# First layer of a two-layer model on one core: the first batch's convolutions moved among all batches' norms, routing and sends in one piece behind them, zeros later, a series fused

## The chip, the core and the metric

The kernel runs on one NeuronCore of one Trainium2 chip, in fp32 throughout. The metric is the device time of one execution in microseconds. The engines are TensorE (PE, with its weight loads PEld), VectorE (DVE), ScalarE (ACT), GpSimd (POOL) and SyncE (SP). Each takes its instructions in order; DMAs are issued from the queues of SP, ACT and POOL.

## What is computed

The input `u` is 8 batches of 512 rows of 256. Two layers follow, each `x + attention(norm(x)) + ffn(norm(x))`:

```
xn = layernorm(x)
# first layer, attention: a two-way state-space block
z, xBC, dt = split(xn @ in_proj_w.T)
dt  = softplus(dt + dt_bias)                # 16 step sizes per row
xBC = silu(causal_conv4(xBC) + conv_b)      # 1024 channels
x, B, C of both directions = split(xBC)
Y   = ssd(x * dt, -exp(A_log) * dt, B, C, chunk=128)     # both directions
y   = (shifted Y of both + x * (x @ fc_D_w.T + D)) * silu(z)
out = rmsnorm(y) * norm_w @ out_proj_w.T
# first layer, ffn: top-1 of 8 experts, each row goes to one
g, e = max, argmax of softmax(xn @ Wr + br)
out += g * (relu(xn @ W1[e] + b1[e]) @ W2[e] + b2[e])
# second layer: attention of 16 heads over a latent k and v with a decay band,
# and a top-2 mixture of 7 experts and a no-op with 512 places each
```

## The kernel before

**First stage.** `steps()` runs `norm_and_project` over the 8 batches. For one batch it takes the statistics of 4 tiles of 128 rows on DVE (L134, L135), the root on ACT (L164) with a Newton step on DVE (L169 to L174), normalises (`xn`, L140), transposes on PE into `xT` (L147, copied out by ACT at L148), multiplies with `w_small` (`pp`, L152) and copies the result into `proj` (L156): 16 step-size columns and 8 router logits. SP loads the batches (`ask`, L304) and stores each `xT` to DRAM (`keep`, L366). ACT's queue writes zeros over the expert rows' array `xd0`, a part per batch (`clear`, L121). Behind the loop come the step sizes: softplus as a series in `z2` (L391 to L406), then `da` (L412). This part and all up to L1050 is put in order by the framework's scheduler, which may interleave what is independent.

**First batch.** `first = batch[0]` loads its `xT` back from DRAM (L741). A convolution (`conv`, L751) is a projection of 128 channels on PE (`pj`, L746), a scaled copy `cv` on ACT (L755), three taps on DVE that read `pj` in PSUM (L759), `th` on ACT (Tanh, L763) and a last product on DVE (L764). There are two `pj` banks. Eight convolutions make `x` (`x_part`) and `bc` (`bc_part`) of a batch. The list `pending` with `slot()` runs the later parts of a convolution at the next call. `decays`, `tokens`, `edges` and the first parts of `chunk[0]` prepare the loop.

**Chunk loop.** 64 chunks follow (8 per batch: 4 in each direction) in an order written out by hand (`tc.manual_schedule`). Per chunk POOL makes `au` (L922), `xdd` (L965), a part of `yT` (L996) and the state (L1008); PE makes `seg` (L938), `yd` (L976), `yoff` (L994), `sp` (L1002); ACT the exponentials (L946, L947, L951); DVE `mt` (L970) and others. `others(n)` adds the next batch's convolutions and the last batch's output. Between these, `fill` takes pieces from one generator:

```
rows, rest = itertools.chain(route0(), blocks()), late()
```

A chunk pulls 4 pieces, the first two of a batch 5, the last eight 6. `route0` has 6 pieces of routing (softmax, first maximum, ranks with two matmuls L208 and L209, places, `slot0` at L442, `w_idx` at L454) and 16 pieces of two sends each: an indirect DMA from POOL's queue writes 128 rows of `xn` to their places in `xd0` (L459). `blocks` has 196 pieces for 39 blocks of 128 rows. Each block gathers its expert's weights with indirect DMAs from POOL's queue (L524), turns its rows (L540) and multiplies (`h_ps` L559, `y_ps` L577). `late` then brings the experts' rows back, makes the second layer's norm and router logits (L603 to L666), batch by batch as batches are finished; what is left of it runs inside the second layer.

**Second layer.** A loop over 128 steps of attention with its expert work between (L1464 on).

The functions that the change touches:

Of the kernel before, what the change touches and what calls it, by code (L numbers as in the profile page):

```python
# [2 lines left out]

# [50 lines left out]
def bc(ap, axis, shape):  # L54

    return ap.unsqueeze(axis).to_broadcast(shape)
# [3 lines left out]
def tile_kernel(ctx: ExitStack, tc: tile.TileContext, t, out: bass.AP):  # L60
# [57 lines left out]
    def clear(dst, rows, lo, hi):  # L118

        n = rows // P  # L120
        A.dma_start(  # L121
            out=dst[: n * P, :].rearrange("(p r) d -> p r d", p=P)[:, lo:hi, :],
            in_=bc(zero[:, : dst.shape[1]], 1, [P, hi - lo, dst.shape[1]]),
        )


    def norm_and_project(x_of, xn, xT_of, w_proj, n_proj, proj, pool, bank):

        for b in range(B):
            x = x_of(b)  # L130
            mv = pool.tile([P, TPB, 2], FP, name="mv", tag="mv")
            for c in range(TPB):
                st = pool.tile([P, 6], FP, name="st", tag="st", bufs=4)
                V.bn_stats(st, x[:, c, :])  # L134
                V.bn_aggr(mv[:, c, :], st)  # L135
            ve = pool.tile([P, TPB], FP, name="ve", tag="ve")
            V.tensor_scalar(ve, mv[:, :, 1], EPS, None, ALU.add)
            rs = rsqrt(pool, ve, [P, TPB])
            for c in range(TPB):
                V.tensor_scalar(  # L140
                    xn[:, b * TPB + c, :], x[:, c, :], mv[:, c, 0:1], rs[:, c : c + 1], ALU.subtract, ALU.mult
                )
            xT = xT_of(b)
            for k in range(KC):
                tp = bank("tp", [P, S], 0)
                for c in range(TPB):
                    T.transpose(tp[:, c * P : (c + 1) * P], xn[:, b * TPB + c, k * P : (k + 1) * P], ident)  # L147
                A.copy(xT[:, k, :], tp)  # L148
            pp = bank("pp", [P, TPB, n_proj], 1)
            for c in range(TPB):  # L150
                for k in range(KC):
                    T.matmul(  # L152
                        pp[:, c, :], xT[:, k, c * P : (c + 1) * P], w_proj[:, k, :],
                        start=(k == 0), stop=(k == KC - 1),
                    )
            V.tensor_copy(proj[:, b * TPB : (b + 1) * TPB, :], pp)  # L156

    def rsqrt(pool, v, shape):

# [201 lines left out]
    def steps():  # L361
# [3 lines left out]
        def keep(b):  # L365
            Y.dma_start(out=xtd[b], in_=xTs[b])  # L366

        def x_of(b):
            if b:
                keep(b - 1)  # L370
            if b >= 2:
                ask(b)

            n = NBLK // B + 1
            clear(xd0, NBLK * P, b * n, min(NBLK, (b + 1) * n))
            if b == 3:
                Y.dma_start(out=w_in, in_=t["w_in"])
            if b == 5:
                Y.dma_start(out=w_out, in_=t["w_out"])
            return us[b]  # L380

        def xT_of(b):
            xTs[b] = m2.tile([P, KC, S], FP, name="xT", tag="xT")
            return xTs[b]

        norm_and_project(x_of, xn, xT_of, w_small, 2 * NH + NE, proj, pool, bank)
        keep(B - 1)

# [6 lines left out]
        V.tensor_tensor(z, z, u, ALU.mult)  # L397
        V.tensor_tensor(z2, z, z, ALU.mult)
        acc = u
        V.tensor_scalar(acc, z2, 1.0 / 17.0, 1.0 / 15.0, ALU.mult, ALU.add)  # L400
        for k in range(13, 0, -2):
            V.tensor_tensor(acc, acc, z2, ALU.mult)
            V.tensor_scalar(acc, acc, 1.0 / k, None, ALU.add)
        V.tensor_tensor(acc, acc, z, ALU.mult)
        V.tensor_scalar(acc, acc, 2.0, None, ALU.mult)
        V.scalar_tensor_tensor(dt.rearrange(f2), v.rearrange(f2), 0.0, acc.rearrange(f2), ALU.max, ALU.add)  # L406
        ea = big.tile([P, 2 * NH], FP, name="ea", tag="ea")
        A.activation(ea, a_log, AF.Exp)
        V.tensor_scalar(ea, ea, -1.0, None, ALU.mult)
# [86 lines left out]
        A.activation(e8, ct, AF.Exp)  # L496
        Y.dma_start(out=exd.rearrange("g p l -> p g l"), in_=e8)

    steps()
    l1c = tl = w_r = rb = w_q = w_o = w_uk = w_uv = w_kv = band = slot1 = iota_n = proj1 = vt0 = qk0 = r1b = noop = None  # L500
    tls = ExitStack()
    for k in range(HC):
        V.tensor_scalar(w_out[:, k, :], w_out[:, k, :], norm_w[:, k : k + 1], None, ALU.mult)

    with ExitStack() as es:
        p1, p2, psum = m1, m2, mp
        H3 = [P, NH, P]
# [512 lines left out]
        def slot(work=None):  # L1020

            new = work() if work else None
            pending[:] = [more for more in [p() for p in pending] if callable(more)]
            if callable(new):
                pending.append(new)


        first = batch[0]
        first.load()
        for q in range(4):  # L1030
            slot(lambda: first.x_part(q))
        slot(), slot()
        first.skip()()
        first.ask(0), first.ask(1)
        for q in range(4):
            slot(lambda: first.bc_part(q))
            if q == 0:
                pending.append(first.start())
        while pending:
            slot()  # L1040
        first.tokens(0)(), first.tokens(3)()
        decays()
        chunk[0].prepare()
        chunk[0].segments()
# [8 lines left out]
        with tc.manual_schedule(engines=ENGINES):  # L1053
# [29 lines left out]
                    put(next_, "tokens", 0), put(next_, "tokens", 3), put(now, "z_part", 3)  # L1083
                return work

            rows, rest = itertools.chain(route0(), blocks()), late()

            def fill(n):
                for _ in range(n):
# [687 lines left out]
```

## Time and profile before

Three executions took 2058.74, 2060.02 and 2069.62 us (median 2060.02). The profiled execution took 2070.49 us, its span is 2068.8 us, and its mean granted TensorE clock 0.942.

| engine | busy us | share of the span | instructions |
|---|---|---|---|
| PE | 1840.4 | 89% | 11760 |
| PE weight loads | 1229.3 | 59% | 11760 |
| DVE | 1436.3 | 69% | 3311 |
| ACT | 1174.8 | 57% | 2536 |
| POOL | 628.1 | 30% | 572 |

The page gives busy time over the whole span, and the kernel is a sequence of stages with different limits, so the windows by stage say more: there the same columns stand for a stretch of time. In a timeline a row has the start and the duration in us, the engine, the line, what is written from what, and in brackets how long the engine stood idle before and what ended that.

Places in time, from the timeline: norm stage 0 to 72.9; step sizes done at 101.3; chunk 0's `yd` at 132.1; sends 150.2 to 206.7; first weight gather at 209.0; last `y_ps` begins at 884; chunk 63's `yd` at 1063; second layer from about 1100.

### The profile page before, as it was taken

How to read it: one execution, taken by the hardware profiler on the slowest of the kernel's cores; microseconds unless marked ns; L12 is line 12 of the kernel's file. 1: busy time of each engine (PE TensorE's matmuls, PEld its weight loads, DVE VectorE, ACT ScalarE, POOL GpSimd, SP SyncE). 2: the span in 40 equal slices, each digit the busy share in tenths (PEclk: the TensorE clock that was granted, in tenths of full speed). 3: DMA queues.
4: the chain of work that ended last, by engine and by line, in shares of the span. 5: the costliest groups of instructions: out<-in, count | busy, mean ns of one | idle time of the engine just before them, and what ended most of it. 6: DMA issues, size and time to landing. Idle time of an engine off the chain costs nothing.

```text
span 2068.8 us, 33318 instructions
## 1 busy us (share of the span) xinstructions
PE 1840.4 (89%) x11760; PEld 1229.3 (59%) x11760; DVE 1436.3 (69%) x3311; ACT 1174.8 (57%) x2536; POOL 628.1 (30%) x572
## 2 busy tenths in 40 slices
PE   5676999999999999987776998899999999999987
PEld 5333676766677677744544554466666666666654
DVE  4684766667485665678655776677777777787785
ACT  2243454545344454545433666677877777777775
POOL 0048644546454454555430034300000000000030
PEclk9877999999999999999776999899999999999999
DMA  7113654655455465543533253332231221213170
GB/s 264 61 46 113 209 200 159 209 182 197 145 187 193 159 218 186 158 130 113 165 127 105 96 174 130 110 98 72 68 102 36 81 79 53 81 54 103 34 163 11
DMA packets 150440, 262.34 MB, mean 127 GB/s; under 512 B 22362, under 2 KB 107213, under 8 KB 138369
## 3 DMA queue, kind: packets, MB, share of 16 engines
q1 hardware_dynamic: 112288, 139.62, 21.2%
q0 software_dynamic: 28512, 110.92, 17.3%
q10 hardware_dynamic: 9472, 9.67, 1.4%
q8 instruction: 93, 1.52, 0.3%
q14 instruction: 75, 0.61, 0.1%
HBM read 188.46 MB, written 76.68 MB: 128 GB/s over the span
## 4 chain that ended last, share of the span: by engine, by line
PE 36%; ACT 7%; DVE 4%; issue 1%; another core or an unknown queue 1%; DMA 1%; ACTq 0%; SPq 0%; DVEq 0%
PE p_ps L1493 8%; PE s_ps L1471 6%; PE o_ps L1502 6%; PE e_yp L1275 5%; PE e_hp L1262 5%; ACT s L1486 3%; ACT pT L1494 2%; PE qp L254 1%; DVE s L1478 1%; DVE s L1476 1%; PE fin L1434 1%; PE vp L269 1%; PE kp L262 1%; PE op L896 0%
## 5 line engine op out<-in xcount | busy, mean ns | idle before, releaser
L1476 DVE TENSOR_SCALAR s<-s_ps 128x512 f32<-128x512 f32 x512 | 318.1, 683 | 208.0 <-PE s_ps L1471 181.1
L1486 ACT ACTIVATE s<-s,ng 128x512 f32<-128x512 f32 x512 | 355.8, 727 | 5.7 <-DVE ng L1482 5.6
L1493 PE MATMUL p_ps<-ident,s 128*128 128x128 f32 x2048 | 288.6, 284 | 53.9 <-ACT pT L1494 48.9
L1478 DVE CUSTOM_DVE_ANT_0 s<-s,band 128x512 f32<-128x512 f32 x512 | 322.6, 685 | 0.0
L1493 PEld LDWEIGHTS p_ps<-ident,s 128*128 128x128 f32 x2048 | 239.0, 144 | 119.8 <-ACT pT L1494 77.5
L1494 ACT COPY pT<-p_ps 128x512 f32<-128x512 f32 x512 | 277.5, 592 | 48.3 <-PE p_ps L1493 39.2
L1281 POOL DMA_INDIRECT x<-e_yo,e_to x28 | 43.4, 1552 | 599.0 <-ACT e_yo L1280 545.8
L746 PE MATMUL pj<-xT,w_in 128*128 128x512 f32 x384 | 203.9, 658 | 17.6 <-DVE cv L759 14.7
L1471 PE MATMUL s_ps<-kT,qT 16*128 16x512 f32 x1024 | 163.6, 674 | 14.2 <-DVE s L1476 9.5
L559 PEld LDWEIGHTS h_ps<-xdT,w 128*128 128x128 f32 x1248 | 149.1, 192 | 22.4 <-issue 21.6
L559 PE MATMUL h_ps<-xdT,w 128*128 128x128 f32 x1248 | 152.7, 276 | 2.9 <-DMA w<-in_w_dram,w_idx 2.9
L759 DVE SCALAR_TENSOR_TENSOR cv<-pj,w_conv_w,cv 128x511 f32<-128x511 f32 (+2 forms) x192 | 143.0, 745 | 11.1 <-ACT cv L755 7.1
L577 PE MATMUL y_ps<-w,hT 128*128 128x256 f32 x624 | 147.3, 380 | 0.0
L922 POOL TENSOR_TENSOR au<-da,half 128x512 f32<-128x512 f32 x64 | 77.9, 1217 | 223.2 <-PE seg L938 121.1
L1502 PE MATMUL o_ps<-pT,vt 128*32 128x256 f32 x2048 | 134.0, 396 | 2.0 <-issue 1.8
L577 PEld LDWEIGHTS y_ps<-w,hT 128*128 128x128 f32 x624 | 115.9, 190 | 31.8 <-issue 17.8
L746 PEld LDWEIGHTS pj<-xT,w_in 128*128 128x128 f32 x384 | 72.1, 206 | 100.5 <-issue 91.4
L996 POOL TENSOR_TENSOR yT<-yT,ex 128x512 f32<-128x512 f32 (+1 forms) x48 | 58.6, 1220 | 222.3 <-DVE ex L995 155.1
L1262 PE MATMUL e_hp<-e_xdT,e_w 128*128 128x256 f32 x448 | 123.3, 398 | 1.5 <-ACT e_xdT L1247 0.7
L1275 PE MATMUL e_yp<-e_w,e_hT 128*128 128x256 f32 x448 | 120.4, 391 | 0.0
L951 ACT ACTIVATE mt<-seg,mid 64x64 f32<-64x64 f32 x512 | 109.8, 309 | 0.8
L763 ACT ACTIVATE th<-cv 128x512 f32<-128x512 f32 x64 | 40.3, 630 | 117.0 <-DVE cv L759 113.2
(296 smaller groups left out, 3046.6 us busy)
## 6 DMA issues: line engine op xcount, KB each, us to landing
ex<-exd SPq DMA_DIRECT2D x96, 128.0 KB
u<-in_u_dram SPq DMA_DIRECT2D x16, 512.0 KB
xtd<-xT SPq DMA_DIRECT2D x16, 512.0 KB
fr<-fdd SPq DMA_DIRECT2D x64, 128.0 KB
xT<-xtd SPq DMA_DIRECT2D x15, 512.0 KB
od<-os SPq DMA_DIRECT2D x28, 256.0 KB
e_w<-in_ei_dram SPq DMA_DIRECT2D x7, 1024.0 KB
e_w<-in_eo_dram SPq DMA_DIRECT2D x7, 1024.0 KB
```

The lines of the kernel that those rows point to most:

```text
L559: T.matmul(hp[:, i, :], w1[:, k * FF + f * P : k * FF + (f + 1) * P], xdT[:, k * P : (k + 1) * P], start=(k == 0), stop=(k == KC - 1),)
L577: T.matmul(yp, hT[f // 4][:, f % 4, :], w2[:, f * DM : (f + 1) * DM], start=(f == 0), stop=(f == FC - 1))
L746: T.matmul(pj, w_in[:, k, o * P : (o + 1) * P], self.xT[:, k, :], start=(k == 0), stop=(k == KC - 1))
L1262: T.matmul(hp, w1[:, k, f * P : (f + 1) * P], xdT[:, k, :], start=(k == 0), stop=(k == KC - 1))
L1275: T.matmul(yp, hT[:, f, c * P : (c + 1) * P], w2[:, f, :], start=(f == 0), stop=(f == FC - 1))
L1471: T.matmul(sp[i], self.q[r, cols], self.k[r, :], start=True, stop=True)
L1476: V.tensor_scalar(self.p[i], sp[i], -CLAMP, CLAMP, ALU.max, ALU.min)
L1478: V.tensor_tensor_reduce(out=self.p[i], in0=self.p[i], in1=band[:, at : at + S], scale=1.0, scalar=-3.0e38, op0=ALU.mult, op1=ALU.max, acc ...
L1486: A.activation(self.p[i], self.p[i], AF.Exp, bias=self.ng[:, i : i + 1])
L1493: T.transpose(pp[:, k, :], self.p[i][:, k * P : (k + 1) * P], ident)
L1494: A.copy(pT[i][:, :, cc * P : (cc + 1) * P], pp)
L1502: T.matmul(op[32 * i : 32 * i + 32, half * 2 * P : (half + 1) * 2 * P], self.v[:, k, h * (AD + 1) : h * (AD + 1) + 32], pT[i][:, k, :], st ...
```

## The change

- `norm_and_project` takes a function `behind(b)` that it calls after each batch. It starts two of batch 0's convolutions behind each of the batches 2 to 5. Batch 0's `xT` stays in SBUF, in a buffer of the tag `yT`, and is not loaded back.
- `route0` runs as a whole inside `steps()`, ahead of the series in the program's text, and no longer in the chunk loop's pieces.
- The zeros over `xd0` come from a tile `none`, in four DMAs behind the norm stage instead of eight in it.
- In the series, each pair of a product and an addition of a constant is one `scalar_tensor_tensor`: seven instructions fewer.
- `w_in` is asked for at batch 1 (batch 3 before, by the text), and the scaling of `w_out`, `skip`, `tokens` of chunks 0 and 3, and `start` are moved in the text.

The scheduler's order of the changed program on POOL in this stretch is: `none`, two `xdt`, 32 sends, two `xdt`, `au`, `xdd`, two `au`, two `xdt`, six weight gathers. On DVE, `slot0` stands near the end of the series, one instruction behind `da`'s first half.

```diff
@@ -124,7 +123,7 @@
         )
 
 
-    def norm_and_project(x_of, xn, xT_of, w_proj, n_proj, proj, pool, bank):
+    def norm_and_project(x_of, xn, xT_of, w_proj, n_proj, proj, pool, bank, behind):
 
         for b in range(B):
             x = x_of(b)
@@ -154,6 +153,7 @@
                         start=(k == 0), stop=(k == KC - 1),
                     )
             V.tensor_copy(proj[:, b * TPB : (b + 1) * TPB, :], pp)
+            behind(b)
 
     def rsqrt(pool, v, shape):
 
@@ -370,21 +370,43 @@
                 keep(b - 1)
             if b >= 2:
                 ask(b)
-
-            n = NBLK // B + 1
-            clear(xd0, NBLK * P, b * n, min(NBLK, (b + 1) * n))
-            if b == 3:
+            if b == 1:
                 Y.dma_start(out=w_in, in_=t["w_in"])
             if b == 5:
                 Y.dma_start(out=w_out, in_=t["w_out"])
             return us[b]
 
         def xT_of(b):
-            xTs[b] = m2.tile([P, KC, S], FP, name="xT", tag="xT")
+            if b == 0:
+                first.xT = xTs[b] = m2.tile([P, HC, S], FP, name="xT0", tag="yT")[:, :KC, :]
+            else:
+                xTs[b] = m2.tile([P, KC, S], FP, name="xT", tag="xT")
             return xTs[b]
 
-        norm_and_project(x_of, xn, xT_of, w_small, 2 * NH + NE, proj, pool, bank)
+        def behind(b):
+
+            for q in range(2 * b - 4, min(2 * b - 2, 2 * HC)) if b >= 2 else ():
+                part = first.x_part if q < HC else first.bc_part
+                slot(lambda: part(q % HC))
+            if b == B - 1:
+                while pending:
+                    slot()
+
+        norm_and_project(x_of, xn, xT_of, w_small, 2 * NH + NE, proj, pool, bank, behind)
         keep(B - 1)
+
+        none = m1.tile([P, TPB, DM], FP, name="none", tag="u", bufs=2)
+        G.memset(none, 0.0)
+        slots = xd0.rearrange("(p r) d -> p r d", p=P)
+        for lo in range(0, NBLK, 3 * TPB):
+            n = min(3 * TPB, NBLK - lo)
+            k = n // 3 if n % TPB else TPB
+            A.dma_start(
+                out=slots[:, lo : lo + n, :].rearrange("p (n k) d -> p n (k d)", k=k),
+                in_=bc(none[:, :k, :].rearrange("p k d -> p (k d)"), 1, [P, n // k, k * DM]),
+            )
+        for _ in route0():
+            pass
 
 
 
@@ -397,13 +419,13 @@
         V.tensor_tensor(z, z, u, ALU.mult)
         V.tensor_tensor(z2, z, z, ALU.mult)
         acc = u
-        V.tensor_scalar(acc, z2, 1.0 / 17.0, 1.0 / 15.0, ALU.mult, ALU.add)
-        for k in range(13, 0, -2):
-            V.tensor_tensor(acc, acc, z2, ALU.mult)
-            V.tensor_scalar(acc, acc, 1.0 / k, None, ALU.add)
-        V.tensor_tensor(acc, acc, z, ALU.mult)
+        acc, z, z2, v = (a.rearrange(f2) for a in (u, z, z2, v))
+        V.tensor_scalar(acc, z2, 1.0 / 17.0, None, ALU.mult)
+        for k in range(15, 1, -2):
+            V.scalar_tensor_tensor(acc, acc, 1.0 / k, z2, ALU.add, ALU.mult)
+        V.scalar_tensor_tensor(acc, acc, 1.0, z, ALU.add, ALU.mult)
         V.tensor_scalar(acc, acc, 2.0, None, ALU.mult)
-        V.scalar_tensor_tensor(dt.rearrange(f2), v.rearrange(f2), 0.0, acc.rearrange(f2), ALU.max, ALU.add)
+        V.scalar_tensor_tensor(dt.rearrange(f2), v, 0.0, acc, ALU.max, ALU.add)
         ea = big.tile([P, 2 * NH], FP, name="ea", tag="ea")
         A.activation(ea, a_log, AF.Exp)
         V.tensor_scalar(ea, ea, -1.0, None, ALU.mult)
@@ -496,12 +518,8 @@
         A.activation(e8, ct, AF.Exp)
         Y.dma_start(out=exd.rearrange("g p l -> p g l"), in_=e8)
 
-    steps()
     l1c = tl = w_r = rb = w_q = w_o = w_uk = w_uv = w_kv = band = slot1 = iota_n = proj1 = vt0 = qk0 = r1b = noop = None
     tls = ExitStack()
-    for k in range(HC):
-        V.tensor_scalar(w_out[:, k, :], w_out[:, k, :], norm_w[:, k : k + 1], None, ALU.mult)
-
     with ExitStack() as es:
         p1, p2, psum = m1, m2, mp
         H3 = [P, NH, P]
@@ -1026,19 +1044,16 @@
 
 
         first = batch[0]
+        steps()
         first.load()
-        for q in range(4):
-            slot(lambda: first.x_part(q))
-        slot(), slot()
+        for k in range(HC):
+            V.tensor_scalar(w_out[:, k, :], w_out[:, k, :], norm_w[:, k : k + 1], None, ALU.mult)
         first.skip()()
         first.ask(0), first.ask(1)
-        for q in range(4):
-            slot(lambda: first.bc_part(q))
-            if q == 0:
-                pending.append(first.start())
+        first.tokens(0)(), first.tokens(3)()
+        pending.append(first.start())
         while pending:
             slot()
-        first.tokens(0)(), first.tokens(3)()
         decays()
         chunk[0].prepare()
         chunk[0].segments()
@@ -1083,7 +1098,7 @@
                     put(next_, "tokens", 0), put(next_, "tokens", 3), put(now, "z_part", 3)
                 return work
 
-            rows, rest = itertools.chain(route0(), blocks()), late()
+            rows, rest = blocks(), late()
 
             def fill(n):
                 for _ in range(n):
```

More of the change, by code (lines that the diff above doesn't have):

```diff
@@ L1 @@
-import itertools
 from contextlib import ExitStack
```

## The prediction

> **What bounds the kernel now.** I read the windows by stage first, to see where TensorE has room, then the timeline of each engine's queue from 0 to 230 us, then the first starts of the groups `yd` (L976, once per chunk) and `y_ps` (L577, once per expert block). Columns: stretch, its length, busy us (instructions) of PE, weight loads, DVE, ACT, POOL, then granted clock, DMA share, GB/s.
>
> ```profile
> 0.00:76.00 76.00, 48.58 (x197) 41.80 (x198) 35.87 (x167) 16.62 (x31) 3.30 (x20) 1.00 0.64 221
> 76.00:101.00 25.00, 12.66 (x21) 3.48 (x19) 24.55 (x40) 5.62 (x9) 0.00 (x0) 0.78 0.01 1
> 101.00:132.00 31.00, 20.82 (x61) 8.85 (x60) 23.80 (x33) 16.36 (x39) 10.19 (x8) 0.78 0.15 47
> 132.00:226.00 94.00, 65.66 (x270) 35.68 (x270) 53.04 (x103) 29.66 (x79) 66.20 (x64) 0.75 0.37 128
> 226.00:889.00 663.00, 649.04 (x3950) 469.36 (x3948) 437.51 (x730) 319.49 (x871) 338.37 (x292) 1.00 0.55 180
> 889.00:1063.00 174.00, 134.99 (x692) 85.06 (x690) 125.64 (x250) 80.43 (x192) 79.98 (x74) 0.86 0.46 141
> ```
>
> From 226 to 889 PE is the bound (98% busy): chunks 6 to 51 at 663/45 = 14.73 us each, with 4.25 pieces of expert work per chunk. After 889 the expert blocks are finished; twelve chunks take 14.5 us each beside the second layer's row work, DVE 72% busy. Before 226 each of the six chunks takes 15.7 us without expert work: POOL, 66.2 of 94 us busy, carries the sends (L459) between its chunk work. All the room for this change is before 226 and, through what moves out of it, after 889; the second layer from 1100 on is untouched.
>
> ```profile
> 64.74 0.26 DVE L156 COPY proj<-pp 128x96 f32<-128x96 f32 x1 [3.46 <-PE pp L152]
> 65.91 1.38 DVE L140 TENSOR_SCALAR xn<-u,mv,rq_r 128x256 f32<-128x256 f32 x4
> 72.62 0.26 DVE L156 COPY proj<-pp 128x96 f32<-128x96 f32 x1 [5.33 <-PE pp L152]
> 100.51 0.76 DVE L412 TENSOR_TENSOR da<-dt,ea 128x256 f32<-128x256 f32 x2
> 132.10 1.98 PE L976 MATMUL yd<-mt,xdt 128*64 128x128 f32 x16 [4.18 <-DVE mt L970]
> 149.71 0.18 DVE L442 CAST slot<-so_sa 128x32 int32<-128x32 f32 x1
> 163.52 0.99 POOL L459 DMA_INDIRECT xd<-xn,slot  x1 [0.17 <-issue]
> 164.82 0.98 POOL L459 DMA_INDIRECT xd<-xn,slot  x1 [0.30 <-issue]
> 208.98 1.06 POOL L524 DMA_INDIRECT w<-in_w_dram,w_idx  x1 [1.24 <-DMA xd<-xn,slot]
> ```
>
> Seen here, in time: a batch's turn in the norm stage is a latency chain of 7.88 us (64.74 to 72.62), 6.7 of it from the start of `xn` to the copy of `proj`. Step sizes are done at 101.3, chunk 0 multiplies at 132.1, slots are known at 149.9, one send occupies POOL for 1.29 us (163.52 to 164.82), and the first weight gather issues at 208.98, after the last send.
>
> **The change part by part**, against this execution. The order of the changed kernel's instructions is known: it interleaves the eight convolutions of batch 0 with the norms of batches 2 to 7, and on POOL it puts two `xdt`, then all 32 sends in one run, and only then chunk 0's `au` and `xdd`.
>
> *Convolutions moved into the norm stage.* One is three taps and a finish on DVE (rows 0.74, spaced 0.66, and 0.69), 0.78 + 0.63 on ACT, 1.9 on PE. DVE gets 8 x 2.6 = 21 us, beside 36 it has there now. The chain does not hide them, because DVE runs in order and they stand between a `proj` copy and the next `xn`. Walking it: batch 2's `u` is asked for behind batch 1's store, at 19 instead of 13.4, and is there by about 27 (8.9 us from issue now); two convolutions with a table load and three waits on ACT put `xn` of batches 2 and 3 at 37 and 39, their `proj` at 43 and 49. Batch 4: five taps 3.3, a finish 0.6, statistics and Newton 2.6, then the 6.7 chain: 62.4. Batch 5: four taps 2.6, 1.5, 6.7, and 1.0 for `fp` matmuls ahead of its `pp`: 74.3. Batch 6: three taps 2.0, statistics, Newton and a `w_out` scaling 3.4, 6.7: 86.5. Batch 7, partly ahead: 6.6, so the stage ends at 93 instead of 73. In return the stretch from 76 to 125, where these convolutions alternated with the series, keeps only the series.
>
> Sqrt and Tanh now alternate, with about ten more table loads on ACT. The row for one is
>
> ```profile
> 7.11 1.28 ACT L408 ACT_TABLE_LOAD   x1
> 8.41 0.22 ACT L408 ACTIVATE ea<-w_a_log 128x16 f32<-128x16 f32 x1
> ```
>
> so 1.30 us from load to use: 13 us on an ACT that has 60 idle there, in the chain only for batches 6 and 7, inside my walk. The Trainium skill ("ScalarE: Activation LUTs", "What ACT_TABLE_LOAD costs") adds a drain of some 1.38 us to each switch. By it up to six `rq_s` would come 1.4 later: +8 us. The trace shows no such gap; I take zero and keep 8 for the range.
>
> *Zeros later.* Eight issues on ACT's queue, 5.1 MB, leave 7 to 32 us; four larger ones go out between about 83 and 91, behind a POOL memset of 128x1024 (0.31 us for 128x272, so 1.2). At the 221 to 287 GB/s seen in the first stage they take 18 to 23 us and are down by about 114, under routing; uncovered they would hold the first send as long as they are late. The early `u` loads gain bandwidth, which only matters for batches 2 and 3, and is in the walk. SP's order changes little: `w_in` keeps its place, batch 0's `xT` is no longer reloaded (0.32 of issue). I put both at zero, bounds -3 and +3.
>
> *Routing and series.* Fusing drops seven `tensor_scalar` of 0.414 (L403): -2.9 us on DVE; STT and TT cost the same (0.683 and 0.680). From 93: softmax and first maximum 5.5, ranks on PE and eviction 2.8, then series and ranks alternate: `sp_v` 0.7 and two exponentials 1.4, the reciprocal 3.35, ten fused steps and products of 0.62 spacing each and some twenty small routing rows of 0.1 to 0.4: about 20. `dt` at 121, `slot` at 122. The kernel before had step sizes at 101 and its last batch-0 convolution at 125: chunk 0 has its inputs at the same time in both.
>
> *Sends directly behind.* After two `xdt` (2.5) the 32 sends take 32 x 1.29 = 41.3: 124 to 165. In the kernel before they cost POOL the same, but spread over chunks 0 to 5. Here `au` waits behind them, and for `au` the segment matmul, its exponentials, `mt`, and `yd`: two `xdt` to 167.6, `au` 168.8, matmul 1.1, exponentials 2.9, `mt` 1.2: chunk 0 multiplies at 174 instead of 132. Three more `au`, an `xdd` and two `xdt`, each on the other engines' leave, bring the first weight gather to 178 instead of 209; its weights land 5.9 us later as now (208.98 to 214.85), at 184. Chunk 1's `yd` stands behind block 0's first matmuls on PE, and comes at about 194.
>
> *Cold TensorE.* PE has next to nothing from 95 to 180. After the similar gap at 1100:
>
> ```profile
> 1110.00:1120.00 10.00, 1.97 (x6) 1.67 (x8) 6.81 (x18) 4.95 (x7) 0.00 (x0) 0.50 0.31 105
> 1120.00:1130.00 10.00, 8.56 (x41) 5.33 (x38) 9.71 (x32) 5.98 (x11) 0.00 (x0) 0.62 0.16 54
> 1130.00:1140.00 10.00, 9.16 (x64) 5.32 (x66) 8.41 (x21) 5.84 (x11) 0.00 (x0) 0.72 0.73 262
> 1140.00:1150.00 10.00, 9.71 (x62) 5.28 (x55) 5.91 (x15) 4.91 (x10) 0.00 (x0) 0.94 0.00 0
> ```
>
> the clock took 30 us to come back: (0.38 + 0.28 + 0.06) x 10 = 7 us of PE lost. The skill ("TensorE: Matmul & The Clock Gate", Part 1) restores it after one busy window of 3.4 us: 1.7 lost. The row is nearer, since chunk 1 has the same mix of bursts: I take 6, bounds 2 and 10. So chunk 1 at 199, and with 14.73 each chunk 6 at 272, against 226: +46.
>
> *What comes back.* Routing and sends were 22 of the pieces that chunks pull (6 and 16). Without them the blocks start with chunk 0 and end at 196/4.25 = chunk 46 instead of 218/4.25 = 51. Five chunks lose their expert work. What is such a chunk worth? From 889 the windows hold 12 bare chunks and six batches of row work. A bare chunk has 8.6 us of DVE by its rows; at the 0.72 to 0.83 filling that row work leaves DVE, 10.4 to 12; two neighbours without row work stand 9 apart (996 and 1005). I take 10.4: 5 x (14.7 - 10.4) = -22, bounds -28 (9.1) and 0 (chunks no shorter, as chunks 0 to 5 were). And batch 6's row work, which now holds PE 6.2 us after the last chunk (1071.8), finds free pieces in chunks 61 to 63: -5, bounds -8 and 0.
>
> Sum: +46 - 22 - 5 = +19, say +20: 2070.5 becomes 2090. The profiled execution is 10.5 above the median of the runs, 2060.0; to that I add the same 20: **2080**.
>
> **The rivals.**
> *Tail no shorter* (25%). Late chunks are bound by waits (DVE for `yd`, PE for `mt`), not by PE, and shedding PE work gives back only a part: -4 to -12 instead of -22. Then +29 to +42, 2090 to 2102; with the drains 2110. For it: without expert work 12 chunks took 14.5 each, not less than with it. Against: they carried six batches of row work.
>
> *A draw* (17%): norm stage done by 84, tail as taken or a bit shorter: +9 or less, 2050 to 2070.
>
> *Faster* (8%): the mixed norm stage costs nothing. PE and DVE are each idle for 27 to 40 us in the first 76, and a third of its DMA bytes leave. If the convolutions fit in those gaps and it ended at 73 as now, everything behind comes 20 earlier: chunk 6 at +26; with the tail at its best, 26 - 28 - 8 = -10, 2050. It decides at a stage end of 73; later than that the run of sends is not paid for. Against: the chain and the order on DVE above.
>
> *The change doesn't do what it says*: the scheduler might have spread the sends. The order on POOL excludes it.
>
> **Numbers.** The likeliest, 50%: +10 to +30, 2070 to 2090. What this kernel's measurement can tell from no change is about 0.5%, 10 us: 2050 and 2070 are the borders. Faster 0.08, same 0.17, slower 0.75. For 8 in 10 I leave out the fastest tenth and the last tenth beyond the uncovered drains: 2054 to 2106.
>
> **What would show it.** Right: last `proj` copy at 85 to 98; `slot` near 122; 32 sends in one run of 41 us with `au` behind it; first `yd` at 165 to 182; first weight gather at 170 to 185; chunk 6 near 272; last `y_ps` near chunk 46, and from there to the last `yd` about 226 us. Wrong: `au` ahead of the sends or a first `yd` under 150; a norm stage under 78; the chunks behind the last block at 9 us or less; or a gain in the second layer, of which I expect nothing.

## The result, and the profile after

The changed kernel takes 2093.39 us (median of four runs, 2086.59 to 2096.63) beside 2061.49 for the kernel before. The ratio is 1.0128, 95% interval 1.0103 to 1.0152: by that ratio 26 us slower. (The two medians lie 31.9 apart; the ratio is what is used below.) A second measurement, on a chip where the kernel before took 2073.91, gave 1.0122 (1.0092 to 1.0152). The profiled execution after took 2086.59 us, with a span of 2084.9, 16.1 longer than the one shown of before; of that pair only the part up to the second layer is used below, for reasons given with the runs of both kernels on one chip.

The windows by stage, of the changed kernel (columns as in the prediction):

```profile
0.00:76.00 76.00, 49.53 (x185) 31.14 (x185) 48.67 (x181) 33.49 (x47) 3.48 (x21) 0.86 0.37 126
76.00:101.00 25.00, 14.32 (x54) 10.97 (x53) 13.31 (x39) 7.86 (x13) 1.09 (x1) 0.50 0.77 289
101.00:132.00 31.00, 9.79 (x31) 5.30 (x30) 25.11 (x55) 3.98 (x8) 13.51 (x13) 0.61 0.28 90
132.00:226.00 94.00, 53.95 (x297) 38.60 (x298) 25.59 (x45) 27.78 (x81) 56.41 (x54) 0.74 0.45 158
226.00:889.00 663.00, 636.03 (x3832) 454.69 (x3831) 439.60 (x723) 308.12 (x842) 339.98 (x296) 0.99 0.54 177
889.00:1063.00 174.00, 127.83 (x619) 74.90 (x618) 119.60 (x242) 87.33 (x197) 65.03 (x57) 0.81 0.35 114
```

DVE's convolution work moved into the first 76 us (48.7 us busy instead of 35.9), and ACT's doubled there. The zeros show in the second row: DMA 77% busy at 289 GB/s. In the fourth row DVE has 25.6 us of work left instead of 53.0, and is idle all the same: up to 159.7 us chunk 0 waits for POOL. The last row is the surprise. As before, it holds only chunks without expert work, eleven of them where there were twelve, and it is hardly emptier.

The timeline of the changed kernel, from DVE, POOL and PE:

```profile
82.67 0.26 DVE L155 COPY proj<-pp 128x96 f32<-128x96 f32 x1 [2.46 <-PE pp L151]
88.62 0.26 DVE L155 COPY proj<-pp 128x96 f32<-128x96 f32 x1 [5.06 <-PE pp L151]
114.27 0.68 DVE L428 SCALAR_TENSOR_TENSOR dt<-sp_v,sp_u 128x512 f32<-128x512 f32 x1
116.35 1.02 DVE L464 CAST slot<-so_sa 128x32 int32<-128x32 f32 x1
117.67 1.72 POOL L481 DMA_INDIRECT xd<-xn,slot  x1 [0.34 <-DVE slot L464]
...
158.72 0.98 POOL L481 DMA_INDIRECT xd<-xn,slot  x1 [0.30 <-issue]
161.69 1.07 POOL L940 TENSOR_TENSOR au<-da,half 128x512 f32<-128x512 f32 x1
...
171.05 1.98 PE L994 MATMUL yd<-mt,xdt 128*64 128x128 f32 x16
174.06 1.09 POOL L542 DMA_INDIRECT w<-in_w_dram,w_idx  x1 [0.15 <-issue]
180.31 3.75 PE L577 MATMUL h_ps<-xdT,w 128*128 128x128 f32 x16 [5.36 <-DMA w<-in_w_dram,w_idx]
```

The norm stage ends at 88.9 instead of 72.9. The sends hold POOL from 117.67 to 159.70, with nothing else between them; `au` of chunk 0 follows, and chunk 0 multiplies at 171 instead of 132. The weights' gather issues at 174 instead of 209.

For chunks, the clearest clock is the one addition of `yd` into `yT` that each of them makes on DVE. Its starts (us), and that of the second layer's first score matmul, for both kernels in the first profiles and in a later pair on one chip:

| | chunk 0 | 6 | 46 | 51 | 63 | second layer | end of span |
|---|---|---|---|---|---|---|---|
| before | 134.1 | 227.2 | 820.6 | 891.4 | 1069.2 | 1102.4 | 2068.8 |
| after | 173.1 | 261.9 | 854.6 | 936.6 | 1112.2 | 1136.8 | 2084.9 |
| before, again | 134.4 | 224.1 | 822.6 | 893.4 | 1073.6 | 1106.6 | 2074.7 |
| after, again | 170.6 | 260.8 | 855.9 | 936.7 | 1108.0 | 1132.0 | 2096.6 |

In the later pair the loss is 36.2 us at chunk 0, 36.7 at chunk 6, 33.3 at chunk 46, 34.4 at chunk 63, 25.4 at the second layer and 21.9 at the end. So the start costs less than the 46 predicted, and the chunks without expert work give nothing back.

### The profile page after: what moved, and what is told of

It reads as the page before. It is cut to its first block, busy times and chain, and to the rows that moved or that the text cites. A ratio compares the mean times of both kernels' runs of the same rounds, so it can differ in the third digit from the quotient of the medians.

```text
span 2084.9 us, 33314 instructions
## 1 busy us (share of the span) xinstructions
PE 1823.4 (87%) x11760; PEld 1216.1 (58%) x11760; DVE 1427.7 (68%) x3304; ACT 1188.4 (57%) x2548; POOL 628.7 (30%) x573
## 4 chain that ended last, share of the span: by engine, by line
PE 37%; ACT 6%; DVE 4%; issue 1%; DMA 1%; POOL 1%; ACTq 0%; another core or an unknown queue 0%; SPq 0%; DVEq 0%; POOLq 0%
PE p_ps L1508 8%; PE s_ps L1486 6%; PE o_ps L1517 6%; PE e_yp L1290 5%; PE e_hp L1277 5%; ACT s L1501 3%; ACT pT L1509 2%; PE qp L254 1%; DVE s L1493 1%; DVE s L1491 1%; PE fin L1449 1%; PE vp L269 1%; PE kp L262 1%; ACT e_hT L1280 0%; PE op L914 0%
## 5 line engine op out<-in xcount | busy, mean ns | idle before, releaser
L777 DVE SCALAR_TENSOR_TENSOR cv<-pj,w_conv_w,cv 128x509 f32<-128x509 f32 (+2 forms) x192 | 142.8, 745 | 8.7 <-ACT cv L773 4.7
L595 PEld LDWEIGHTS y_ps<-w,hT 128*128 128x128 f32 x624 | 115.9, 190 | 33.3 <-issue 18.7
L988 DVE TENSOR_TENSOR mt<-mt,cbm 128x1024 f32<-128x1024 f32 x64 | 82.4, 1287 | 41.9 <-ACT mt L969 41.7
```

Of the source, the lines that this page charges most:

```text
L595: T.matmul(yp, hT[f // 4][:, f % 4, :], w2[:, f * DM : (f + 1) * DM], start=(f == 0), stop=(f == FC - 1))
```

## The experiments

They ran on several chips, on which the kernel before took from 2041 to 2075 us, so only ratios to the kernel before on the same chip are compared, and starts up to the second layer.

**The run of sends.** `e1_sends_spread` leaves routing in front, and lets the chunks pull the sends again:

```
-        for _ in route0():
-            pass
+        sends = route0()
+        for _ in range(6):
+            next(sends)
...
-            rows, rest = blocks(), late()
+            rows, rest = itertools.chain(sends, blocks()), late()
```

> The changed kernel, with the 32 sends pulled by the chunks again, two to a piece (routing stays in front). Theory (the run of sends holds POOL ahead of chunk 0's au): the first yd comes 41 us earlier, at 130 instead of 171, chunk 6 near 228 instead of 261, blocks end near chunk 50; time about 2058, ratio 0.995 to 1.003 to the kernel before. Rival (chunk 0 is late because TensorE is cold or because the zeros' transfers hold everything behind them): the first yd at 145 or later, time 2075 or more.

Measured: ratio 1.0014 (1.0005 to 1.0022). POOL's and PE's timelines of this kernel:

```profile
118.98 1.48 POOL L943 TENSOR_TENSOR au<-da,half 128x512 f32<-128x512 f32 x1
133.29 1.23 POOL L484 DMA_INDIRECT xd<-xn,slot  x1 [0.19 <-issue]
...
130.26 1.97 PE L997 MATMUL yd<-mt,xdt 128*64 128x128 f32 x16 [0.45 <-DVE mt L991]
```

`au` now stands ahead of the first send, and `yd` comes at 130.3 instead of 171. The zeros were as late (issued between 77 and 87 us, and between 78 and 88 in the changed kernel). TensorE was a little warmer: its granted clock was 0.74 from 115 to 125 us and 0.69 from 125 to 130. In the changed kernel it was 0.50 from 160 to 171, where TensorE was busy for 5.1 us, so the clock is worth 2.5 us there at most. Neither is what held chunk 0 for 41 us; the run on POOL is. It accounts for 1.1% of the changed kernel's 1.3%, some 22 us. Chunk 6 comes at 231.5 and not at 228, still 30 earlier than after.

**Routing as well.** `e2_route_spread` puts routing back into the chunks too, so that only the mixed convolutions, the late zeros and the fused series are left of the change:

```
-        for _ in route0():
-            pass
...
-            rows, rest = blocks(), late()
+            rows, rest = itertools.chain(route0(), blocks()), late()
```

> The changed kernel, with routing and sends both pulled by the chunks again, as in the kernel before; mixed convolutions, late zeros and fused series stay. Theory (behind the norm stage DVE is the path, and routing is half of it there): dt near 104 instead of 114, the first yd near 118 instead of 171 and 132 in the kernel before, chunk 6 near 213, the rest as in the kernel before: time about 2046, ratio 0.990 to 0.996. Rival (the first chunks are bound by POOL's sends and by routing, whenever chunk 0 starts; what is won there is waited out before the first block): first yd early, chunk 6 at 224 or later, ratio 0.998 to 1.003.

Measured: 0.9945 (0.9926 to 0.9963), the first `yd` at 120.71, chunk 6 at 214.6. The theory holds: behind the norm stage DVE is the path. `dt` is done at 103 instead of 114 in `e1_sends_spread`, because DVE has 19 operations from the last copy of `proj` to `dt` instead of 61: routing no longer alternates with the series. Chunk 0 wins 9.6 us by it and chunk 6 16.9, and that is still there at the second layer (17.5): routing in front costs 0.7%.

**The mixing, undone.** `e3_convs_behind` keeps routing and sends in front and calls batch 0's convolutions behind the norm stage, as in the kernel before:

```
-            for q in range(2 * b - 4, min(2 * b - 2, 2 * HC)) if b >= 2 else ():
-                part = first.x_part if q < HC else first.bc_part
-                slot(lambda: part(q % HC))
...
+        for q in range(4):
+            slot(lambda: first.x_part(q))
...
+        for q in range(4):
+            slot(lambda: first.bc_part(q))
```

> The changed kernel, with batch 0's convolutions behind the norm stage again; routing and run of sends stay in front. Theory (the mixing moves DVE work, it doesn't hide it): the last proj copy at 73 instead of 89, but 21 us of convolution stand between routing's and the series' operations, so the slots come at 120 to 128 and the first yd at 172 to 182; ratio 1.012 to 1.020. Rival (the mixing costs the norm chain more than the convolutions cost behind it): slots by 112, first yd by 166, ratio under 1.010.

Measured: 1.0124 (1.0104 to 1.0143), as slow as the changed kernel. Half of each guess was right: the ratio is the theory's, the slots are the rival's. They came at 103, and the sends ran from 103.43 to 145.65. Yet the first `yd` came at 168.45, only 2.6 earlier than after. ACT's and DVE's timelines say why:

```profile
145.72 1.04 POOL L934 TENSOR_TENSOR au<-da,half 128x512 f32<-128x512 f32 x1
148.94 0.60 ACT L958 ACTIVATE mt<-seg 128x512 f32<-128x512 f32 x1 [24.60 <-PE seg L950]
...
153.09 0.63 ACT L775 ACTIVATE th<-cv 128x512 f32<-128x512 f32 x1
153.75 0.69 DVE L776 SCALAR_TENSOR_TENSOR bc<-th,cv 128x512 f32<-128x512 f32 x1 [24.84 <-ACT th L775]
```

The scheduler had put chunk 0's exponentials ahead of the last convolutions' `th` on ACT. The exponentials wait 24.6 us for `seg`, that for `au`, that for the sends, and the convolutions stand behind them. One engine's in-order wait became another's. With the run of sends in place, then, it is worth nothing to mix or not to mix.

**The parts by themselves.** `e7_mix_only` is the kernel before with the mixed convolutions alone; `e8_no_mix` is it with the late zeros and the fused series alone. The edit of the first, with what `behind` needs of the change (`w_in` asked for with batch 1, a tile of its own for batch 0's `xT`, the calls that were moved in the text; nearly all of this is in `e8_no_mix` too):

```
-        norm_and_project(x_of, xn, xT_of, w_small, 2 * NH + NE, proj, pool, bank)
+        norm_and_project(x_of, xn, xT_of, w_small, 2 * NH + NE, proj, pool, bank, behind)
```

and of the second:

```
-            clear(xd0, NBLK * P, b * n, min(NBLK, (b + 1) * n))
...
+        none = m1.tile([P, TPB, DM], FP, name="none", tag="u", bufs=2)
+        G.memset(none, 0.0)
...
-            V.tensor_tensor(acc, acc, z2, ALU.mult)
-            V.tensor_scalar(acc, acc, 1.0 / k, None, ALU.add)
+            V.scalar_tensor_tensor(acc, acc, 1.0 / k, z2, ALU.add, ALU.mult)
```

> The kernel before, with batch 0's convolutions mixed into the norm stage and nothing else of the change (zeros early, series unfused, routing and sends in the chunks). Theory (the mixing is the part that gains where nothing holds chunk 0 up behind it: it takes 21 us of DVE from behind the norm stage and puts 14 in front): first yd near 125 instead of 132, ratio 0.996 to 0.998. Rival (early zeros and mixed convolutions collide on ACT's queue and on the early loads, so that the norm stage ends past 92): ratio 0.999 to 1.003.

> The kernel before, with late zeros and the fused series but the convolutions behind the norm stage, routing and sends in the chunks. Theory (seven tensor_scalar less on DVE and nothing else): first yd at 127 to 130 instead of 132, ratio 0.997 to 1.000. Rival (the late zeros are still under way when the first send needs them): sends later than 163, ratio over 1.001.

Measured: mixing 0.9950 (0.9931 to 0.9969), the rest 0.9997 (0.9983 to 1.0011); together they make the 0.9945 of `e2_route_spread`. The mixing gains 0.5%, more than the 0.2 to 0.4% expected, and is the only part that gains: the norm stage ends later, at 82 instead of 72 to 73, and chunk 0 starts earlier, its addition at 120.5 instead of 134.4. In `e8_no_mix` `dt` is ready at 94 instead of 100, but the last convolution finishes on DVE at 124.9 (125.6 before), so chunk 0 is only 2 us early: a shorter series is worth nothing where the convolutions end later than it.

Beside these two, the norm stage of `e2_route_spread` ended at 86.9, not at 82. With late zeros the scheduler places the convolutions among the norms in another order (on DVE the two orders part in the second batch), and that took back what fusing saved. So `e12_mix_fused` is the mixing and the fused series with early zeros; against `e2_route_spread`:

```
-        none = m1.tile([P, TPB, DM], FP, name="none", tag="u", bufs=2)
-        G.memset(none, 0.0)
...
+            n = NBLK // B + 1
+            clear(xd0, NBLK * P, b * n, min(NBLK, (b + 1) * n))
```

> The kernel before with two parts of the change, the mixed convolutions and the fused series; zeros stay early, routing and sends stay in the chunks. Theory (the last two runs: with early zeros the mixed norm stage ends at 82, with late ones at 87, which is as much as the fused series saves): both savings add here, dt at 96 to 98 instead of 102, the first yd at 113 to 117, ratio 0.990 to 0.994 to the kernel before. Rival (what chunk 0 wins is waited out in the first chunks, on POOL's sends and behind routing): first yd as said, chunk 6 no earlier than 213, ratio 0.994 to 0.997.

Measured: 0.9921 (0.9904 to 0.9937), 16 us below the kernel before and the lowest ratio of all versions. DVE and PE of it, and below them DVE of `e7_mix_only`:

```profile
80.74 0.26 DVE L156 COPY proj<-pp 128x96 f32<-128x96 f32 x1 [5.06 <-PE pp L152]
96.40 0.69 DVE L420 SCALAR_TENSOR_TENSOR dt<-sp_v,sp_u 128x512 f32<-128x512 f32 x1
113.77 1.80 PE L986 MATMUL yd<-mt,xdt 128*64 128x128 f32 x16 [3.27 <-DVE mt L980]
```

```profile
81.72 0.26 DVE L156 COPY proj<-pp 128x96 f32<-128x96 f32 x1 [5.06 <-PE pp L152]
101.63 0.69 DVE L420 SCALAR_TENSOR_TENSOR dt<-sp_v,sp_u 128x512 f32<-128x512 f32 x1
```

Behind a mixed norm stage the series is the path, and fusing it takes 4.2 us off: from the end of the last copy to the end of `dt` it is 16.1 us instead of 20.3. Chunk 46 comes at 804.7 instead of 811.5. The ratio's interval just overlaps that of `e7_mix_only`, so the whole time alone does not show the step; the starts do. It overlaps that of `e2_route_spread` as well: that early zeros are better than late ones here is likely, not shown.

**The chunks at the end.** The prediction let five more chunks lose their expert work and become 4.3 us shorter each. `e4_bare_tail` is the changed kernel with all row work (the second layer's norms and router logits, made batch by batch) held back until the last chunk is through:

```
             def fill(n):
                 for _ in range(n):
-                    if next(rows, "end") == "end":
-                        next(rest, None)
+                    next(rows, None)
...
             slot()
+            for _ in range(80):
+                next(rest)
             batch_done = B
```

> The changed kernel, with the second layer's row work of batches 0 to 6 held back until the last chunk is through, so that the chunks behind the last expert block (47 to 63) carry nothing else. Theory of the prediction (a bare chunk costs 10.4 us): from chunk 46 to chunk 63 about 180 us instead of 257. Rival (the chunks have a chain of their own that is as long with or without other work, some 14 to 15 us): 235 us or more. The whole time grows by the uncovered row work, 50 to 120 us.

Measured, in one run: 163.5 us from chunk 46 to chunk 63, where the theory had 180; chunk 47 comes at 868.0, chunk 63 at 1018.1. The additions on DVE of chunks 47 to 49 and 63:

```profile
868.01 0.68 DVE L1003 TENSOR_TENSOR yT<-yT,yd 128x508 f32<-128x508 f32 x1
876.25 0.68 DVE L1003 TENSOR_TENSOR yT<-yT,yd 128x512 f32<-128x512 f32 x1
884.73 0.69 DVE L1003 TENSOR_TENSOR yT<-yT,yd 128x512 f32<-128x512 f32 x1 [2.07 <-PE yd L994]
...
1018.15 0.68 DVE L1003 TENSOR_TENSOR yT<-yT,yd 128x508 f32<-128x508 f32 x1 [0.69 <-PE yd L994]
```

A chunk that carries nothing else, a bare chunk, takes 150.1/16 = 9.4 us, less than the prediction's 10.4. The rival that a chunk's own chain is 14 us long is out. The windows of this kernel show what becomes of the row work by itself:

```profile
868.00:1018.00 150.00, 122.71 (x677) 70.36 (x675) 109.04 (x152) 78.40 (x213) 76.71 (x62) 0.95 0.18 54
1018.00:1147.00 129.00, 68.32 (x274) 51.96 (x275) 54.88 (x180) 24.20 (x41) 36.15 (x39) 0.61 0.57 182
```

It takes 128.5 us from the last chunk to the second layer (1018.1 to 1146.6), at a clock of 0.61. No engine is busy for more than 53% of it, so none of them sets its length by itself. And bare chunks and row work one after the other take little longer than side by side. From chunk 46 to the second layer it is 292 us here, and 282 and 276 in the two profiles of the changed kernel, where the same row work lies beside the chunks. Only 10 to 16 of its 128 us were hidden there.

The whole time was 2080.9 on a chip where the kernel before took 2042.4. Against the changed kernel, at its ratio of 1.0122 to 1.0128, that is a growth of some 13 us, where I had expected 50 to 120 from row work in the open.

`e5_rows_from_52` lets the row work begin with chunk 52, close to where it began in the kernel before:

```
-                    if next(rows, "end") == "end":
+                    if next(rows, "end") == "end" and late_from <= 0:
                         next(rest, None)
...
+                late_from = 52 - n
```

> The changed kernel, with the second layer's row work allowed to start with chunk 52 only, near where it started in the kernel before; chunks 47 to 51 are bare. Theory (row work costs a chunk its slack whenever it is there, some 15 to 16 us a chunk for 4 pieces or for 6; without it a chunk takes 9.4, as the held-back run showed): chunks 46 to 51 take 47 to 55 us instead of 82, the next twelve as many as in the kernel before (178); time 18 to 30 us below the changed kernel, ratio 0.998 to 1.005 to the kernel before. Rival (each piece of row work costs about 1 us wherever it is put): what chunks 47 to 51 win is paid later, ratio 1.009 to 1.014.

Measured: 1.0189 (1.0174 to 1.0205). My theory fell. Chunks 46 to 51 took 52.4 us instead of 82, as it said, but the next twelve took 195.5 instead of 176, the end behind them 33.6 instead of 24.6, and the second layer began at 1136.7, where it began after. All that the bare chunks won was paid later, and some more: the ratio is 0.6% above the changed kernel's. Against `e8_no_mix`, traced on the same chip and as fast as the kernel before, the second layer begins 32.7 us later; the pair of before and after on one chip, below, has 25.4 there. Of these 7 us, 5 lie between chunk 46 and the second layer (281.5 us, and 276.1 in that pair); the rest of the 0.6% is not explained.

`e6_dense_tail` is `e2_route_spread` with the row work from chunk 56 on and eight pieces a chunk:

```
-                if n >= N - 8:
-                    fill(2)
+                if n >= N - 8:
+                    fill(4)
...
+                late_from = N - 8 - n
```

> The version with routing and sends in the chunks (mixed convolutions, late zeros, fused series), with the row work allowed to start with chunk 56 only and then at eight pieces a chunk instead of six. Theory (a chunk that carries row work takes some 15 us whether it carries 4, 6 or 8 pieces): chunks 52 to 55 shrink from 15 to 10 us each, the rest stays: 15 to 22 us below that version, ratio 0.984 to 0.988 to the kernel before. Rival (cost by the piece): chunks 56 to 63 grow to 17 to 18 us each and eat it: ratio 0.993 to 0.997.

Measured: 1.0061 (1.0042 to 1.0080), 1.2% worse than `e2_route_spread`. Chunks 52 to 56 shrank to 11.0 us each, and chunks 56 to 63 grew from 14.9 to 21.4, more than the rival's 17 to 18: both guesses missed. Crowded into eight chunks, row work is hidden less than in twelve.

Is it TensorE's wait for the row work's `xn`? `e9_rows_apart` is the changed kernel with two empty pieces more between `xn` and its transposes:

```
                 ahead(3)
                 yield
+                if b < 6:
+                    yield
+                    yield
```

> The changed kernel, with two empty pieces more between the normalised rows xn and the transposes that read them, in the row work of batches 0 to 5. Theory (in the tail, TensorE stands in its order before transposes whose xn is not ready, 21 us in all, and the chunks behind it stand too; that wait makes row work cost as much beside chunks as by itself): PE's wait for xn falls under 8 us, chunks 46 to 63 take 258 less 15 to 20 us, ratio 0.992 to 0.995 of the changed kernel, so 1.004 to 1.009 to the kernel before. Rival (another engine's order, or the cold clock, is what holds the chunks; the wait moves elsewhere): the wait for xn goes, the chunks take 250 us or more, ratio 1.010 to 1.016.

Measured: 1.0089 (1.0057 to 1.0121), beside 1.0122 for the changed kernel on the same chip. The waits from chunk 46 to 63, of the changed kernel and then of this one (us in total, times, longest):

```profile
PE tp L672 <- DVE xn L664: 20.9, 5, 9.4
POOL au L940 <- PE seg L956: 51.5, 9, 15.6
```

```profile
PE tp L675 <- DVE xn L664: 14.1, 4, 10.4
POOL au L943 <- PE seg L959: 48.9, 9, 21.9
```

The wait shrank by 6.8 us, not to under 8, and the stretch by 3.4 (248.7 instead of 252.1). The intervals overlap, so a gain is not shown. Two thirds of the wait are left, so it is not ruled out either, but a third of it gone gave back 3.4 us. POOL's wait for the segments, and with it the next chunk's `au`, stayed.

**Both kernels on one chip.** `e10_before_again` and `e11_after_again` are the two kernels themselves.

> The kernel before itself, for a trace beside those of the experiments. Theory (the second layer is untouched): from the second layer's first score matmul to the end 933 to 940 us, as in the experiments on this chip, not 966 as in the first profile; chunks as in the first profile. Rival (the change's gain of some 18 us in the second layer between the first two profiles is real): 950 us or more.

> The changed kernel itself, beside the experiments on their chip. Theory: ratio 1.010 to 1.015 again, and the second layer 933 to 940 us long. Rival (the first ratio was that chip's): ratio under 1.008.

Measured: from the first score matmul to the end of the span 968.1 us before and 964.6 after; `e9_rows_apart` on the same chip has 962.8. The 933 to 940 that I wrote down held for `e1_sends_spread`, `e2_route_spread` and `e3_convs_behind` on theirs (934.8, 934.9, 936.6). So that length goes with the chip (or with the hour: each chip was used once), and hardly with the kernel: within a chip it differs by 5.3 us at most. In the first two profiles it was 966.4 and 948.1, which made the changed kernel look 18 us better there. Before and after on one chip show 3.5. The ratio was confirmed.

## Why the prediction was right or wrong, point by point

- **Forecast.** 2080 was forecast and 2093.39 measured, inside the range of 2054 to 2106 and just beyond the likeliest 2070 to 2090; as a difference, 20 and 26. The direction rests on the right cause, the run of sends. That the size fits is luck. In the pair on one chip, the front was taken 9 us too dear (+46 for +36.7 at chunk 6) and the tail 23 too cheap (-22 for +1.1), and three small terms came out better than forecast: 3.4 us in the expert blocks, 4.0 in batch 6's row work, 3.5 in the second layer.
- **The walk through the norm stage** said `proj` copies at 43, 49, 62.4, 74.3, 86.5 and 93 for batches 2 to 7. They came at 43.6, 47.1, 59.6, 70.4, 82.7 and 88.6. (The steps given for batch 4 add up to 62.2; nothing hangs on it.) That DVE's order makes the stage longer was right. From a copy of `proj` to the next batch's `xn` it took 5.7, 3.9 and 4.8 us in front of batches 4, 5 and 6, with DVE busy all the time from 60 to 65 us and for 4.6 of the 5 us from 70 to 75; in the kernel before it was 0.5 to 2.0. The granted clock fell too, to 0.50 from 75 us on, where the kernel before had 1.00, but the stage's matmuls do not show it. The last batch's `pp`, before and after:

```profile
68.91 3.67 PE L152 MATMUL pp<-w_w_small,xT 128*128 128x24 f32 x16 [0.51 <-ACT xT L148]
```

```profile
84.92 3.67 PE L151 MATMUL pp<-w_w_small,xT 128*128 128x24 f32 x16 [0.51 <-ACT xT L147]
```

  The rival of a stage that ends at 73 is out. In the second profile it ended at 87.
- **Table loads.** ACT has 14 in the first 90 us instead of 4: ten more, as said. One of the new ones:

```profile
29.16 1.28 ACT L781 ACT_TABLE_LOAD   x1
30.46 0.63 ACT L781 ACTIVATE th<-cv 128x512 f32<-128x512 f32 x1
31.77 1.28 ACT L164 ACT_TABLE_LOAD   x1
33.07 0.20 ACT L164 ACTIVATE rq_s<-ve 128x4 f32<-128x4 f32 x1
```

  Each is 1.30 us from its start to the next instruction's, and there is no drain behind it. Taking zero of the 8 us, the estimate from the drain that the Trainium skill ("ScalarE: Activation LUTs", "What ACT_TABLE_LOAD costs") adds to each switch, was right.
- **Routing and series**: `slot` at 116.4 and `dt` at 114.3, forecast 122 and 121. Four of those six to seven us are the norm stage's, which ended at 88.9 instead of 93.
- **The run of sends**: 42.0 us forecast as 41.3, from 117.7 instead of 124; first `yd` 171 for 174, first weight gather 174 for 178. This is the step that decides, and `e1_sends_spread` shows that it does.
- **Zeros**: issued between 78 and 88 instead of 83 and 91, and down by about 100 instead of 114 (the DMA share is 0.76 from 96 to 100 us and 0.02 from 100 to 104); the first send waited 0.34 us, for the slots. Zero was right for the transfer. Not foreseen was that without their early issues the scheduler mixes the convolutions differently. One detail was wrong, also in the account of the change: batch 0's `xT` is loaded again (SP issues it at 86.8), at 0.32 us.
- **Cold TensorE and the first chunks.** Here the front was taken too dear. The windows of the changed kernel:

```profile
160.00:170.00 10.00, 4.08 (x8) 1.04 (x8) 1.22 (x1) 2.89 (x10) 4.79 (x5) 0.50 0.17 52
170.00:180.00 10.00, 4.95 (x32) 4.09 (x30) 2.21 (x3) 4.51 (x14) 8.11 (x7) 0.67 0.43 145
180.00:190.00 10.00, 9.69 (x46) 7.57 (x47) 1.13 (x4) 3.55 (x9) 6.29 (x8) 0.77 0.88 343
190.00:200.00 10.00, 10.00 (x63) 7.46 (x62) 5.89 (x10) 4.89 (x15) 3.59 (x4) 1.00 0.39 132
```

  The clock is whole within 10 to 20 us of the first block's start at 180.3. Lost are 0.33 of the 5 us busy in the second row and 0.23 of the 9.7 in the third, 4 us in all, and 2 more in the first row, ahead of that block: close to the 6 taken, and between the two estimates of 1.7 and 7. Chunk 6 was forecast at 272 and came at 261: 3 us of that lead are there at chunk 0 (171 for 174), 4 more at chunk 1 (192 for 199), and the rest are chunks of 13.7 us instead of 14.73 ((261.9 - 193.3)/5).
- **"Five chunks lose their expert work: -22"** is the step that failed, and not by its unit price. A bare chunk does cost 9.4 us. The prediction's reading of 9, from the `yd` at 996 to the one at 1005, agrees with it by luck: these two are not without row work. TensorE has in between

```profile
997.49 0.81 PE L654 MATMUL tp<-ident,xn 128*128 128x128 f32 x4
999.25 1.85 PE L661 MATMUL pp<-w_w_r,xT 128*128 128x8 f32 x16
```

  and their additions on DVE are 16.3 us apart. Yet, for all that price, from chunk 46 to chunk 63 the changed kernel took 252 to 258 us, where 226 was forecast, and the kernel before 249 to 251: the term is +1 to +9 instead of -22. TensorE's work did leave (between chunk 46 and the second layer it was busy for 197 to 205 us instead of 227 to 232), but waiting took its place. The error was to count the row work as something that lies in a chunk's slack at a fixed price. Take the stretch from the end of the blocks to the second layer, less what the bare chunks took in `e4_bare_tail`. In the kernel before that leaves 211 to 213 - 111 = 100 to 102 us for row work and the end; in the changed one 276 to 282 - 163.5 = 113 to 119; by itself the work takes 128. So 26 to 28 us of it were hidden before, and 10 to 16 after. The number of chunks that it is spread over is not the whole reason: `e5_rows_from_52` has nearly the twelve chunks of the kernel before, and hides as little as the changed one (229 - 111 = 118). `e5_rows_from_52` and `e4_bare_tail` show that moving it about leaves the sum where it was, within 16 us. Why it does not lie beside the chunks better is open. The clock is not what differs: TensorE's busy time times the share of the clock not granted, summed over windows of 10 us from chunk 46 to the second layer, is 27 and 30 us in the two profiles of the kernel before, 35 and 26 in those of the changed one, and 31 in `e4_bare_tail`. TensorE's wait for `xn` is at most a part, and POOL's order was not tried by itself. The rival "tail no shorter", to which I gave 25%, is what happened there, and more than that: it still took 4 to 12 us off the tail.
- **Batch 6's row work: -5** was -9.0 in the pair on one chip: 24.0 us from the last chunk to the second layer instead of 33.0.
- **The second layer** gains nothing, as forecast; the first two profiles alone would have said otherwise.

## What to carry to other kernels

An in-order queue makes a run of cheap instructions as expensive as its length for whatever stands behind it: here 42 us of sends, and chunk 0 41 us later. The sends had to be done anyway; issued in one run ahead of the first chunk's `au` they cost 1.1% of the whole kernel more than when the chunks pull them two at a time. When work is moved from a busy stage to one with spare time, measure the second stage bare before pricing the move: low busy shares in it do not mean that the work will fit, and here the times of row work and chunks nearly added up.

A change of several parts is worth taking apart. Here the mixing gains 0.5%, the fused series gains only on top of it, and routing and sends in front lose 1.8% together; the first two by themselves are 0.8% faster than the kernel before.

## What was not expected of the hardware

- The same program differs by 1.7% between chips (the kernel before: 2041 to 2075 us), and nearly all of it is in the second layer. The changed kernel reaches chunk 46 at 855.9 us on one chip, and `e4_bare_tail`, whose code is the same up to there, at 854.6 on another; the second layer takes 933 to 937 us on two chips and 963 to 968 on two others, whatever the kernel (the two first profiles have 966 and 948). The granted clock from 1180 to 2020 is 0.98 to 0.99 on the former and 0.97 on the latter; by an estimate, 840 us times a difference of 0.01 to 0.02, that alone is some 8 to 17 us of the 30, and the rest is not explained.
- Row work by itself ran at a granted clock of 0.61 over 129 us, with TensorE busy for 53% of it: here half-idle TensorE was not granted its full clock.
- A lower clock did not lengthen every matmul: `pp` of a batch, 16 matmuls of 24 columns, took 3.67 us at 1.00 and at 0.50.
